# Two transformer blocks: the normed inputs move from VectorE to ScalarE, under a new work order

## The chip, the cores and the metric

The kernel runs on one core of a Trainium2 chip. A core has five engines with a queue of instructions each: TensorE (PE in the profile; PEld is its loading of weights), VectorE (DVE), ScalarE (ACT), GpSimd (POOL) and SyncE (SP), which here issues all DMAs. Each queue runs in order, and an instruction that waits for another engine holds up everything behind it. The metric is the device time in microseconds, as the median of several runs. Three runs of the kernel before gave 1454.73, 1455.28 and 1455.34 us.

## The reference, cut to what matters

A batch of 32 sequences of 128 tokens with 256 features goes through two blocks, all in fp32. Each block is self attention, cross attention to a context, and a feed-forward part of width 1024, with 16 heads of 16 features. In front of each of the three parts the input is normed over its features:

```python
m = jnp.mean(x, axis=-1, keepdims=True)
v = jnp.mean((x - m) ** 2, axis=-1, keepdims=True)
return (x - m) / jnp.sqrt(v + EPS)
```

Most of these normed inputs are then scaled by a factor `1 + scale` and shifted, both taken from a condition vector. There are 6 norms for each sequence, three in each block.

## The kernel before

The 32 sequences are handled as 16 groups of two (`GB = 2`), so a tile of inputs `x` is 128 tokens by 2 x 256. Every group goes through both blocks. Eight streams (`NS`) are under way at once, each with one group, so that while one stream waits for a transfer or for a softmax the products of another run. Five sets of query, key and value tiles (`NA`), three tiles for normed inputs (`y`), four tiles of PSUM for products and a single one for scores are shared by all the streams.

The order of the work is not the order of the code. A planner in the kernel (`Clock` and `Tasks`) runs while the program is built. Every step of a stream is a Python generator that yields when it can start, on which engine and with which shared tiles. The planner keeps a time for each engine, picks the step to issue next, and adds the cost that the step states with `clock.use`. In each stretch of 40 us of planned time the number in `ORDER` decides how long it holds back for a step of better rank, and stirs the ranks. So the costs in `clock.use` and the numbers in `ORDER` decide the order in which the instructions of all streams stand in each engine's queue. On the chip these queues are fixed, and the engines wait for one another by semaphores. They do not keep the planned times.

The steps that the prediction speaks of are these:

- **The norm** (`normed_T`, L565 to L588). VectorE takes the mean and variance `mv` of each sequence with bn_stats and bn_aggr (L572, L573). GpSimd adds eps (L577) and raises to the power -0.5 (L579), which gives `rstd`. Two operations, one for each sequence, then write the normed tile `y` (L586). TensorE transposes it in four pieces (`transposed`, L598), and ScalarE or VectorE, whichever is planned to be free first, scales and shifts it out of PSUM into the stream's tile `xt` (L616 on ScalarE, L618 on VectorE).
- **Attention** (`attention`, from L751). For each sequence TensorE computes the scores (L761), VectorE takes the largest of each row (L773), TensorE transposes these (L786), VectorE subtracts them from the queries (L790, tile `qa`), TensorE computes the scores anew (L761), ScalarE takes the exponential (L799), and TensorE multiplies by the values (L807). ScalarE copies the result to a tile `ou` (L813), some of whose rows hold the sums of the exponentials.
- **The division by the sums** (`over_sums`, L818 to L842). The sums go by DMA to a tile `few` (L825), the other rows to `xt` (L827), VectorE inverts `few` (L830), the inverses go by DMA to DRAM (L833) and by two more DMAs back to where they are needed (L838), and VectorE multiplies (L841). After this come the output projection (`project`, with `w_sa_out_w` or `w_ca_out_w`) and the sum with `x` (L881, or L885 and L889 where there is a gate).
- **Setting up** (`set_up`, L391). ScalarE fills the five sets' query and key tiles, ten copies of 128 x 1024, once, at the start.
- **Products** (`multiply`, L273 and L275). A product with a weight is one matmul of 128 columns, or four of 32 columns, where the planner finds TensorE already working in parts.

Of the kernel before, what the change touches and what calls it, by code (L numbers as in the profile page):

```python
# [10 lines left out]
F32 = mybir.dt.float32  # L11
U8 = mybir.dt.uint8
AF = mybir.ActivationFunctionType
ALU = mybir.AluOpType
# [3 lines left out]
P = 128  # L18
B, S, D, H, HD, DF = 32, 128, 256, 16, 16, 1024
KC = D // P  # L20
FC = DF // P
GB = 2
# [10 lines left out]

EVERY = 40.0
ORDER = (
    38718, 32014, 0, 87893, 99950, 56838, 0, 53341, 21925, 7768, 6954, 0, 63578, 91846, 41557, 5424, 0, 45477, 0,
    75801, 0, 86349, 57432, 99928, 14485, 81598, 5044, 38730, 0, 40902, 37263, 32089, 83999, 84738, 0, 0, 0
)


# [201 lines left out]
def two_blocks(ctx: ExitStack, tc: tile.TileContext, a: dict, out: bass.AP):  # L242
    nc = tc.nc

    def pool(name, bufs, **kw):
        return ctx.enter_context(tc.tile_pool(name=name, bufs=bufs, **kw))
# [5 lines left out]
    clock = Clock()  # L252
# [14 lines left out]
    p_s = pool("p_s", NS + 2)  # L267
# [297 lines left out]
    def normed_T(wm, x, ready, eps, mod, g, name):  # L565


        mv = p_s.tile([P, GB, 2], F32, tag="mv", name=f"mv_{name}")
        yield ready, "dve", "", 1
        for b in range(GB):  # L570
            st = p_s.tile([P, 6], F32, tag="st", name=f"st_{name}_{b}")
            nc.vector.bn_stats(st, x[:, b, :])  # L572
            nc.vector.bn_aggr(mv[:, b, :], st)  # L573
        t = clock.use("dve", 1.17)
        yield t, "pool", "", 1
        ve = p_s.tile([P, GB], F32, tag="ve", name=f"ve_{name}")
        nc.gpsimd.tensor_scalar(ve, mv[:, :, 1], eps, None, ALU.add)  # L577
        rstd = p_s.tile([P, GB], F32, tag="rstd", name=f"rstd_{name}")
        nc.gpsimd.tensor_tensor(rstd, ve, neg_half, ALU.pow)  # L579
        t = clock.use("pool", 1.0)  # L580
        yield t, "dve", "y", 0
        y = clock.take("y")
        xn = ys[y]
        for b in range(GB):

            nc.vector.scalar_tensor_tensor(xn[:, b, :], x[:, b, :], mv[:, b, 0:1],  # L586
                                           rstd[:, b:b + 1].to_broadcast([P, D]), ALU.subtract, ALU.mult)
        t = clock.use("dve", 0.75)  # L588
        return (yield from transposed(wm, y, t, mod, g))

    def transposed(wm, y, t, mod, g):
        to, xn = wm.xt, ys[y]
        yield (lambda: when(t) if mod is None or mod in mods else NEVER), "pe", "mm", 1
        slot = clock.take("mm")
        ps = mms[slot].rearrange("p (c b s) -> p c b s", c=KC, s=S)
        for c in range(KC):
            for b in range(GB):
                nc.tensor.transpose(ps[:, c, b, :], xn[:, b, c * P:(c + 1) * P], ident)  # L598
        t = clock.use("pe", 0.45, "turned")
        clock.give("y", y, t)  # L600
        there = Event()

        def evict():

            engine = "act" if mod is None else clock.freer("act", "dve")
            yield t, engine, "", 1
            if mod is None:
                nc.scalar.copy(to.rearrange("p c (b s) -> p c b s", s=S), ps)
            else:
                scale, shift = mods[mod]  # L610
                for c in range(KC):
                    for b in range(GB):
                        at = g * GB + b
                        one, by, to_add = to[:, c, b * S:(b + 1) * S], scale[:, c, at:at + 1], shift[:, c, at:at + 1]
                        if engine == "act":
                            nc.scalar.activation(one, ps[:, c, b, :], AF.Identity, bias=to_add, scale=by)  # L616
                        else:
                            nc.vector.tensor_scalar(one, ps[:, c, b, :], by, to_add, ALU.mult, ALU.add)  # L618
            clock.give("mm", slot, there.add(clock.use(engine, 0.6 if mod is None else 1.45)))

        tasks.spawn(evict(), wm)
        return there
# [128 lines left out]
    def attention(wm, hd, masked, t, t_v, name, done):  # L751
# [66 lines left out]
        def over_sums():  # L818


            n, w = 4 * R, 4 * H * GT // P
            yield copied, "sp", "", 1
            o = ous[ou[0]]
            few = p_s.tile([P, w], F32, tag="few", name=f"few_{name}", bufs=3)
            nc.sync.dma_start(out=few, in_=o[1:P:8, :, :])  # L825
            at = clock.dma(2.0)
            nc.sync.dma_start(out=wm.xt, in_=o[0:P:2, :, :])  # L827
            clock.dma(2.4)
            yield at, "dve", "", 1
            nc.vector.reciprocal(few, few)  # L830
            yield clock.use("dve", 1.15), "sp", "", 1
            inv = dram2.tile([n, C * GT], F32, tag="inv", name=f"inv_{name}")
            nc.sync.dma_start(out=inv.rearrange("r (t w) -> (r t) w", w=w), in_=few)  # L833
            yield clock.dma(1.5), "sp", "", 1
            by = o[:, 0:KC, :]
            for c in range(2):
                half = inv[:, c * KC * GT:(c + 1) * KC * GT]
                nc.sync.dma_start(out=by[c:P:2, :, :], in_=half.unsqueeze(1).to_broadcast([n, 4, KC * GT]))  # L838
                at = clock.dma(2.3)
            yield at, "dve", "", 1.5  # L840
            nc.vector.tensor_tensor(wm.xt, wm.xt, by, ALU.mult)  # L841
            clock.give("ou", ou[0], done.add(clock.use("dve", 0.7)))  # L842

        copied = Event(GB)
        for b in range(GB):
            tasks.spawn(batch(b), wm)
        tasks.spawn(over_sums(), wm)
        yield last, "none", "", 0
        return last
# [97 lines left out]
    def attended(wm, at, x, masked, t, t_v, w, bias, gate, eps, mod, g, name, then, cx=None):  # L947

        done = Event()
        end = yield from attention(wm, heads[at], masked, t, t_v, name, done)  # L950
        if cx is not None:
            tasks.spawn(cx.fetch(wm), wm)
        if masked:
            end = yield from mask_row(heads[at], zeros, 0)
        clock.give("set", at, when(end))
        if gate is not None:
            gate = yield from load_gate(wm, gate, g)
        t = yield from project(wm, x, lambda k, b: wm.xt[:, k, b * S:(b + 1) * S], KC, w, done, bias, gate, name)
        return (yield from normed_T(wm, x, t, eps, mod, g, then))
# [55 lines left out]
    def stream(wm, mine, loaded):  # L1015

        while loaded:
            first, g = wm.group < NG, wm.group % NG
            x, tx = loaded
            t = yield from normed_T(wm, x, tx, 1e-6 if first else 1e-5, ("L0", "sa") if first else ("L1", 1), g,  # L1020
                                    f"{'a' if first else 'd'}{g}")
            t = yield from (first_block if first else second_block)(wm, x, t, g)
# [125 lines left out]
```

## Time and profile before

| | |
|---|---|
| Median of three runs | 1455.28 us |
| Profiled execution, whole time | 1451.29 us |
| Its span, first to last instruction | 1449.5 us |
| Granted TensorE clock, mean | 0.995 |
| TensorE busy | 98% of the span |
| VectorE busy | 62% |
| ScalarE busy | 48% |
| GpSimd busy | 25% |
| Norm, write of `y` on VectorE (L586) | 192 operations, 128 x 256 each, median 480 ns |
| Inverse deviation on GpSimd (L577, L579) | 96 of 217 ns and 96 of about 705 ns, medians |

The profile is of one execution. The durations of single instructions and the waits are read from it, and they add up to its span. A busy TensorE is not a TensorE at its peak, since matmuls are pipelined and their ends are modelled. The chain of work that ended last runs 82% of the span over TensorE:

```profile
PE 82%; DVE 6%; DMA 5%; issue 2%; POOL 2%; ACT 1%; SPq 1%; DVEq 0%; ACTq 0%; POOLq 0%
```

The idle time of an engine other than TensorE costs nothing by itself. It matters where TensorE waits for that engine.

### The profile page before, as it was taken

The page shows a single profiled execution, that of the slowest core. Times are in us where ns is not written, and L with a number is a line of the kernel's source. Part 1 is how long each engine was busy: PE and PEld are TensorE (multiplying, and loading weights), DVE is VectorE, ACT ScalarE, POOL GpSimd, SP SyncE. Part 2 cuts the span into 40 slices and gives each one's busy share as a digit, 9 for nine tenths or more (in the row PEclk, how much of TensorE's full clock was granted, in tenths as well). Part 3 has the DMA queues.
Part 4 walks back from the last instruction along what each step waited for, and adds up shares of the span by engine and source line. Part 5 has one row for each costly group of instructions (what it writes and reads, how often), then busy time and mean ns, then how long its engine had stood idle before and what let it go on. Part 6 is the DMA issues. An engine that isn't in the chain of part 4 may idle for free.

```text
span 1449.5 us, 45874 instructions
## 1 busy us (share of the span) xinstructions
PE 1422.2 (98%) x20160; PEld 1124.9 (78%) x20160; DVE 900.0 (62%) x1546; ACT 701.1 (48%) x1120; POOL 363.6 (25%) x498
## 2 busy tenths in 40 slices
PE   8999999999999999999999999999999999999998
PEld 7777788777878787787877877778778777768777
DVE  6766656755665565647456665886486567684541
ACT  6554545555446444554455354444444444445542
POOL 3222223213314232424223221222221112210111
PEclk9999999999999999999999999999999999999999
DMA  7432213313132313223322422231121121321110
GB/s 224 155 93 88 72 57 103 100 50 105 46 90 75 108 59 104 89 60 111 99 71 75 151 75 82 85 103 61 60 81 64 56 89 53 96 83 45 42 53 22
DMA packets 107384, 120.91 MB, mean 83 GB/s; under 512 B 11632, under 2 KB 82992, under 8 KB 107184
## 3 DMA queue, kind: packets, MB, share of 16 engines
q1 hardware_dynamic: 107184, 117.98, 25.8%
q8 instruction: 158, 2.59, 0.7%
q14 instruction: 42, 0.34, 0.1%
HBM read 54.92 MB, written 12.68 MB: 47 GB/s over the span
## 4 chain that ended last, share of the span: by engine, by line
PE 82%; DVE 6%; DMA 5%; issue 2%; POOL 2%; ACT 1%; SPq 1%; DVEq 0%; ACTq 0%; POOLq 0%
PE products L275 42%; PE scores L761 16%; PE products L273 13%; PE products L807 7%; PE products L598 3%; DVE top L773 2%; PE products L786 1%; DVE y L586 1%; ACT exp L799 1%; DMA few_b<-ou 1%; DVE qa L790 1%; DMA ou<-inv_b 1%; POOL x L867 1%; POOL gb_a L866 1%; DVE st L736 0%
## 5 line engine op out<-in xcount | busy, mean ns | idle before, releaser
L773 DVE TENSOR_REDUCE top<-scores 128x8 f32<-128x1024 f32 x256 | 300.4, 1215 | 66.8 <-PE scores L761 58.9
L799 ACT ACTIVATE exp<-scores 128x1024 f32<-128x1024 f32 x256 | 248.4, 1023 | 150.5 <-PE scores L761 144.2
L275 PE MATMUL products<-w_ffn_w,ht 128*128 128x256 f32 x896 | 202.4, 381 | 0.0
L275 PEld LDWEIGHTS products<-w_ffn_w,ht 128*128 128x128 f32 x896 | 167.6, 190 | 23.6
L905 ACT ACTIVATE ht<-products,cols 128x256 f32<-128x256 f32 x256 | 115.7, 474 | 115.8 <-PE products L275 84.0
L275 PE MATMUL products<-xt,w_ffn_w 128*128 128x256 f32 x720 | 165.2, 382 | 0.5 <-ACT xt L616 0.5
L761 PEld LDWEIGHTS scores<-qa,keys 32*128 32x128 f32 x4096 | 125.9, 186 | 46.0 <-issue 19.8
L813 ACT COPY ou<-products 128x512 f32<-128x512 f32 x128 | 75.4, 589 | 178.0 <-PE products L807 177.7
L761 PEld LDWEIGHTS scores<-keys,queries 32*128 32x128 f32 x4096 | 126.6, 187 | 37.8 <-issue 21.9
L761 PE MATMUL scores<-qa,keys 32*128 32x128 f32 x4096 | 150.2, 283 | 4.4 <-ACT exp L799 1.6
L761 PE MATMUL scores<-keys,queries 32*128 32x128 f32 x4096 | 151.1, 284 | 2.6 <-ACT exp L799 1.3
L275 PEld LDWEIGHTS products<-xt,w_ffn_w 128*128 128x128 f32 x720 | 134.2, 191 | 20.9 <-ACT xt L616 1.3
L807 PE MATMUL products<-exp,values 128*32 128x128 f32 x4096 | 136.5, 275 | 0.2 <-ACT exp L799 0.2
L741 POOL TENSOR_TENSOR st<-st 128x512 f32<-128x512 f32 x64 | 83.6, 1309 | 204.8 <-DVE st L736 204.8
L790 DVE TENSOR_TENSOR qa<-queries,products 128x512 f32<-128x512 f32 x128 | 86.4, 677 | 72.7 <-PE products L786 55.5
L807 PEld LDWEIGHTS products<-exp,values 128*32 128x32 f32 x4096 | 105.7, 109 | 18.9 <-issue 6.0
L881 DVE TENSOR_TENSOR x<-products,x 128x512 f32<-128x512 f32 x64 | 43.9, 686 | 120.1 <-PE products L275 97.8
L275 PE MATMUL products<-xt,w_qkv_w 128*128 128x256 f32 x408 | 99.4, 389 | 0.8 <-DVE xt L618 0.8
L889 POOL TENSOR_TENSOR x<-y,x 128x512 f32<-128x512 f32 x32 | 41.1, 1285 | 216.2 <-DVE y L885 216.2
L656 ACT COPY values<-products 128x512 f32<-128x512 f32 x64 | 40.4, 632 | 111.8 <-PE products L275 62.8
L841 DVE TENSOR_TENSOR xt<-xt,ou 128x512 f32<-128x512 f32 x64 | 46.2, 723 | 74.5 <-DMA ou<-inv_e 20.6
L736 DVE TENSOR_TENSOR st<-products,rope 128x512 f32<-128x512 f32 x128 | 81.3, 679 | 7.8 <-ACT ou L813 3.3
(129 smaller groups left out, 1958.0 us busy)
## 6 DMA issues: line engine op xcount, KB each, us to landing
xt<-ou SPq DMA_DIRECT2D x64, 256.0 KB
keys<-st SPq DMA_DIRECT2D x96, 128.0 KB
queries<-st SPq DMA_DIRECT2D x96, 128.0 KB
cxt<-in_ctx SPq DMA_DIRECT2D x32, 256.0 KB
x<-in_x SPq DMA_DIRECT2D x16, 256.0 KB
keys<-st SPq DMA_DIRECT2D x16, 256.0 KB
y<-gate_dram_sa SPq DMA_DIRECT2D x16, 256.0 KB
ou<-inv_a SPq DMA_DIRECT2D x32, 128.0 KB
```

The lines of the kernel that those rows point to most:

```text
L273: nc.tensor.matmul(to[j:j + 32], lhsT=lhs[:, j:j + 32], rhs=rhs, start=start, stop=stop)
L275: nc.tensor.matmul(to, lhsT=lhs, rhs=rhs, start=start, stop=stop)
L736: nc.vector.tensor_tensor(st[:, :, :, one], ps[:, :, one].unsqueeze(2).to_broadcast([P, 2, 2, S]), rope, ALU.mult)
L741: nc.gpsimd.tensor_tensor(st[:, 0], st[:, 0], st[:, 1], ALU.add)
L761: nc.tensor.matmul(sc[:, r, c * S:(c + 1) * S], lhsT=lhs(slice(32 * r, 32 * r + 32), c), rhs=rhs(slice(32 * r, 32 * r + 32), c), start=Tru ...
L773: nc.vector.tensor_reduce(top[:, r:r + 2, TOP:TOP + 2 * C:2], scs[slot][:, r:r + 2, :].rearrange("p r (c s) -> p r c s", s=S), AX.X, ALU.max)
L790: nc.vector.tensor_tensor(qa, q[:, :, cut], ps.unsqueeze(1).to_broadcast([P, C, S]), ALU.subtract)
L799: nc.scalar.activation(exps[pt][r // 2], scs[slot][:, r:r + 2, :], AF.Exp, scale=SCALE)
L807: nc.tensor.matmul(mms[at][32 * r:32 * r + 32, c * S:(c + 1) * S], lhsT=v[:, b, i:i + HD, :].rearrange("p d t -> p (d t)"), rhs=exps[pt][r ...
L813: nc.scalar.copy(ous[ou[0]][:, :, cut], mms[at].rearrange("p (c s) -> p c s", s=S))
L841: nc.vector.tensor_tensor(wm.xt, wm.xt, by, ALU.mult)
L905: nc.scalar.activation(ht[f // (FC // 2)][:, f % (FC // 2), :], ps[:, 0, :], AF.Gelu, bias=b1[:, f:f + 1])
```

## The change

There are three edits. First, the normed tile is written by ScalarE in place of VectorE. ScalarE's activation computes `func(scale * x + bias)` with one scale and one bias for each row, so `(x - mean) * rstd` is written as `rstd * x + (-mean * rstd)`. GpSimd works out the bias `nmr`, with two more small operations, and the step's stated costs follow (1.45 for GpSimd, 0.9 for ScalarE). Second, the stated cost of the reciprocal in `over_sums` goes from 1.15 to 1.0; no instruction changes there. Third, the numbers in `ORDER` are others. Through the planner the second and third edits, and the costs of the first, change the order of the instructions in all queues.

```diff
 ORDER = (
-    38718, 32014, 0, 87893, 99950, 56838, 0, 53341, 21925, 7768, 6954, 0, 63578, 91846, 41557, 5424, 0, 45477, 0,
-    75801, 0, 86349, 57432, 99928, 14485, 81598, 5044, 38730, 0, 40902, 37263, 32089, 83999, 84738, 0, 0, 0
+    66186, 45635, 0, 5614, 0, 97056, 0, 0, 45817, 0, 76306, 2557, 0, 5440, 68618, 56612, 0, 0, 5688, 98877, 44020,
+    42862, 35677, 88006, 530, 79523, 1240, 10900, 26993, 41257, 0, 57405, 7496, 0, 55418, 19974, 0
 )
...
         rstd = p_s.tile([P, GB], F32, tag="rstd", name=f"rstd_{name}")
         nc.gpsimd.tensor_tensor(rstd, ve, neg_half, ALU.pow)
-        t = clock.use("pool", 1.0)
-        yield t, "dve", "y", 0
+        nmr = p_s.tile([P, GB], F32, tag="nmr", name=f"nmr_{name}")
+        nc.gpsimd.tensor_scalar(nmr, mv[:, :, 0], -1.0, None, ALU.mult)
+        nc.gpsimd.tensor_tensor(nmr, nmr, rstd, ALU.mult)
+        t = clock.use("pool", 1.45)
+        yield t, "act", "y", 0
         y = clock.take("y")
         xn = ys[y]
         for b in range(GB):
-
-            nc.vector.scalar_tensor_tensor(xn[:, b, :], x[:, b, :], mv[:, b, 0:1],
-                                           rstd[:, b:b + 1].to_broadcast([P, D]), ALU.subtract, ALU.mult)
-        t = clock.use("dve", 0.75)
+            nc.scalar.activation(xn[:, b, :], x[:, b, :], AF.Identity, bias=nmr[:, b:b + 1], scale=rstd[:, b:b + 1])
+        t = clock.use("act", 0.9)
         return (yield from transposed(wm, y, t, mod, g))
...
             nc.vector.reciprocal(few, few)
-            yield clock.use("dve", 1.15), "sp", "", 1
+            yield clock.use("dve", 1.0), "sp", "", 1
```

## The prediction

> **What bounds the kernel now.** I read the page's busy shares first, then TensorE's waits, then the timelines of the places that these point to.
>
> ```profile
> PE 1422.2 (98%) x20160; PEld 1124.9 (78%) x20160; DVE 900.0 (62%) x1546; ACT 701.1 (48%) x1120; POOL 363.6 (25%) x498
> ```
>
> TensorE is busy for 1422.2 of 1449.5 us, so only 27.3 us can be won or lost by anything that does not change TensorE's own stream. Of these, 3.6 us lie at the start (1.35 + 1.46 + 0.82 in the timeline of the first 12 us) and about 4 after the last product (it ends at 1445.5; an add and a store follow). Some 19.7 us in the middle remain, of which the waits by engine name 18.1. The largest are:
>
> ```profile
> PE products L598 <- DVE y L586: 5.4, 8, 1.5
> PE products L275 <- DVE xt L841: 4.9, 5, 1.9
> PE scores L761 <- ACT exp L799: 2.9, 4, 1.1
> PE products L786 <- DVE top L778: 1.7, 4, 0.6
> PE scores L761 <- DVE qa L790: 1.5, 1, 1.5
> PE scores L761 <- DVE top L773: 1.2, 3, 0.6
> ```
>
> (microseconds in total, times, longest.) The change moves exactly L586, so its first line is what it can remove: 5.4 us, of which 1.46 belong to the start. But the second half of the change, a new ORDER, replaces the order of every instruction, so all the other lines are dealt anew.
>
> **What the Trainium skill says.** (1) "ScalarE: Activation LUTs", section "What ACT_TABLE_LOAD costs": an ACTIVATE with a pointer bias takes about 280 ns + 0.833 ns per element, 93 more for a second pointer operand, and neighbours overlap by 93. For 256 columns with bias and scale pointers that is 586 ns alone and, as an estimate, 0.49 apiece in a row. The trace agrees: L682, the same form on 256 columns out of PSUM, has a mean of 566 ns. (2) The same page, "Table sets: the hidden batching unit", has identity in every set. In the trace 228 Identity evictions of L616 and L682 share ScalarE with 32 + 32 loads for exp and gelu alone, so the new ones bring no load. (3) "SBUF — State Buffer", "Who interferes with whom": a VectorE operation with two SBUF inputs contends with GpSimd reads, and ScalarE waits on no one. The trace agrees: L586 has a median of 480 ns but a mean of 509 to 656 by group, and this pair, beside a bias add of GpSimd, took 1.82 us in place of 0.88:
>
> ```profile
> 1403.37 1.82 DVE L586 SCALAR_TENSOR_TENSOR y<-x,mv_f,rstd_f 128x256 f32<-128x256 f32 x2 [1.13 <-POOL rstd_f L579]
> ```
>
> **The change, part by part.**
>
> *TensorE's stream.* The compiled instruction orders of the two kernels, set side by side, hold the same products. The new one issues about as many of them in four 32-column parts (2056 matmuls of that form against 2096), and that would cost nothing, since four parts take as long as one whole product (0.216 us a pass either way, start to start in the timeline). A turn between forms costs 0.1 us from whole products to scores, 0.1 back, 0.11 out of parts or exp products, 0 from exp products to parts; counted with these, the turns of the old order come to 50.1 us and of the new to 50.9. **+0.7.**
>
> *VectorE loses* 192 operations, 106.7 us (15.0+19.5+19.7+17.0+18.6+16.9 in the groups of L586), and takes 16 more evictions (140 for 124) of 0.34: 900 becomes about 799. *ScalarE gains* 192 x 0.49 = 94, and sheds 16 evictions (6 us) and 6 table loads of 1.283 (7.7; 29 + 29 in the new order): 701 becomes about 781. *GpSimd* gains 192 tiny operations. The multiply by -1 is of L577's kind (217 ns, next one 0.30 later); a 128x2 product is not in the trace: between 0.22 (L577) and 0.70 (the pow of L579), I take 0.25, that is 0.6 for the pair and 58 us in all on an engine that is 75% idle. SyncE issues the same 567 rows in another order.
>
> *The norm's chain* is thus 0.6 (GpSimd) + about 0.1 (a pair of 0.98 against 0.88 unhindered) longer, and shorter by up to 0.9 where GpSimd stood in the way. What counts is the queue ahead of y: reductions of 2.35 us before, exps of 1.94 now. I placed each kernel's TensorE order on a line with the pitches above, and asked for each y whether the last reduction (or exp) ahead of it, plus what lies between, ends in time for L598. Shortfalls add to 3.6 us before (3.9 measured after the start) and 0.6 now: **-3.0**. Behind a y that waits for its nmr stand exps, gelus and evictions on ScalarE, and TensorE's next scores or products behind them; 0.97 a time where nothing covers it. I take nothing for it, since reductions lose the same 0.98 behind y on VectorE today.
>
> *The start.* In the new ScalarE order six fills of queries and keys (L391) stand ahead of the first y. They run from 5.40, 0.945 apart:
>
> ```profile
> 5.40 1.04 ACT L391 COPY queries<-rows 128x1024 f32<-128x1024 f32 x1 [2.54 <-DMA rows<-in_rows]
> 6.35 1.04 ACT L391 COPY keys<-rows 128x1024 f32<-128x1024 f32 x1
> ```
>
> So y begins at 5.40 + 6 x 0.945 = 11.07, its first half is there at 11.65, and the first transposition, which came at 9.23 behind VectorE's y of 8.70, moves by **+2.45**. Nothing else is there for TensorE to do: the same 12 warm-up products and modulations stand ahead of it.
>
> *The round of scores.* The same question for reduction to transposition, to the next scores, to qa, and exp to its products: shortfalls sum to 13.9 before and 18.6 now, neighbours counted twice. Several lie between 36 and 70 us and at 766, 1004 and 1064; before they lay around 1250. I take under half of the difference: **+2**.
>
> *The sums' round trip* (L825 to L841) has no cover but other streams' products. Its latency, from the last exp product to the multiplied xt, I read from all 64 cases: the shortest are 9.2, 9.8 and five of 10.0 to 10.2, the lower quartile is 11.7. One that stalled:
>
> ```profile
> 1247.31 0.69 DVE L841 TENSOR_TENSOR xt<-xt,ou 128x512 f32<-128x512 f32 x1 [2.30 <-DMA ou<-inv_d]
> ```
>
> ```profile
> 1241.78 1.08 PE L807 MATMUL products<-exp,values 128*32 128x128 f32 x32
> ...
> 1248.14 1.19 PE L275 MATMUL products<-w_sa_out_w,xt 128*128 128x256 f32 x2 [1.91 <-DVE xt L841]
> ```
>
> (L841 waited 2.30 us for its DMA, and TensorE 1.91 for L841.) The other edit tells the planner that L830 takes 1.0 in place of 1.15 (0.94 measured). In the old order the least work between exp products and projection is 10.5, 10.7 and then 11.9 us; in the new 8.9, 9.0, 9.4, 9.7, 9.8, 10.3, 10.5, and eight more below 11.4. At a latency of 10.2 five of them fall short, by 1.3+1.2+0.8+0.5+0.4: **+4.2**. At 9.2 it would be 0.5, at 11.7 it would be 17 more than before. I take 10.2, about the mean of the seven shortest, since these were the ones with nothing in their way.
>
> *VectorE's relief elsewhere.* L841's 4.9 us of waits came at places with room for 10.5 or more, so from queues on VectorE, GpSimd or SyncE. With 11% less on VectorE I take **-1.5**; no row shows it, between 0 and -4.
>
> Sum: 0.7 - 3.0 + 2.45 + 2 + 4.2 - 1.5 = **+4.9**; 1449.5 becomes 1454.4. The profiled execution took 1451.3 in all, and the median of the runs is 1455.3, 5.8 above the span; so 1460.3, say **1460**.
>
> **The rivals.**
> *Faster.* VectorE's relief is the whole story: the norm's 3.9 us go, half of L841's 4.9, and the 3.4 lost to exp and top (L799, L773) from 1276 to 1309, where the new order has no such pile of scores; start and turns cost 3.15. That is -6.6, **1449**. It holds if the sums' trip stays at 9.2 to 9.4 where it is short of cover, and decides from there. For: VectorE is named for 13.2 of 18.1. Against: nearly all short covers got shorter.
> *No change.* Gaps move, their sum doesn't; what the norm gives back, start and turns take: 0.7+2.45-3.0 = 0, **1455.5**.
> *Slower by more.* The trip takes its quartile of 11.7 also where it is short: 17 us, of which a third is shared with other waits; with the rest of the sum, less its 4.2, that is about +12, **1467**. For: queues on SyncE (DMAs of other streams ahead of L833 and L838) are as before.
>
> **How the numbers follow.** Forecast (+2.9 to +9) 0.40, slower by more 0.14, no change 0.20, faster 0.26. A measurement here tells about 0.2% (2.9 us). Faster 0.26, same 0.20, slower 0.54. The forecast's own range is 1458 to 1465; to leave out no more than 2 in 10, 1449 to 1468.
>
> **What would show it.** In the profile after: L598's first start near 11.65; waits on y near 1 us after the start; no VectorE y at all; ScalarE near 781 busy, VectorE near 799, 58 table loads for exp and gelu; TensorE's busy time within 2 us of 1422; and "products L275 (or L273) <- DVE xt L841" as the largest wait, at 8 us or more. If that line stays below 5 us, the forecast is wrong and the faster rival right; if the start is not late, the six fills did not stand in y's way.

## The result, and the profile after

The kernel after the change takes 1464.77 us in the median of seven runs (1460.75 to 1469.46), beside 1455.93 (1454.73 to 1460.12) for seven runs of the kernel before on the same chip. The ratio is 1.0059, with a 95% interval of 1.0041 to 1.0077. It is slower by 0.6%, where the forecast was 0.3%.

The profiled execution took 1466.39 us with a span of 1464.3, so it lies 1.6 above the median, while the one of before lay below its own. The two spans differ by 14.8 us, the medians by 8.8. What follows accounts for the 14.8, so its parts hold for these two executions, and together they are 6 us more than the medians show. First the busy times, from the page of after:

```profile
PE 1423.7 (97%) x20100; PEld 1127.4 (77%) x20100; DVE 804.6 (55%) x1370; ACT 779.4 (53%) x1290; POOL 393.9 (27%) x690
```

TensorE's own work is nearly what it was (1422.2). VectorE lost 95 us and ScalarE gained 78, as reckoned. So the time went into waits of TensorE. This is the view of TensorE's waits after the change (total, times, longest):

```profile
PE products L275 <- DVE xt L842: 9.2, 8, 2.5
PE products L599 <- ACT y L588: 6.4, 5, 4.3
PE scores L762 <- DVE top L774: 3.6, 5, 1.9
PE products L273 <- DVE xt L842: 3.0, 3, 1.5
PE products L787 <- DVE top L774: 2.9, 4, 1.1
PE products L275 <- ACT ht L906: 2.2, 2, 1.4
PE scores L762 <- DMA queries<-st: 1.7, 1, 1.7
PE scores L762 <- DMA keys<-st: 1.5, 3, 0.8
PE products L273 <- ACT ht L906: 1.0, 1, 1.0
PE scores L762 <- ACT exp L800: 0.7, 2, 0.5
```

(The write of y is L588 now, in place of L586, and line numbers behind it are one higher than in the kernel before.) Set against the waits of before:

| What TensorE waits for | before, us | after, us |
|---|---|---|
| first y of the kernel | 1.5 | 4.3 |
| other y | 3.9 | 2.1 |
| xt, at the end of the sums' round trip | 4.9 | 12.2 |
| round of scores: top, qa, exp | 7.8 | 7.5 |
| gelu output or its release of a PSUM tile (ht) | 0.5 | 3.2 |
| queries and keys by DMA | 0.4 | 3.2 |
| TensorE busy | 1422.2 | 1423.7 |

The differences add to 15.0 us of the 14.8. Half of it is the round trip alone.

The timeline of the longest wait on the trip shows its legs:

```profile
1022.97 1.06 PE L808 MATMUL products<-exp,values 128*32 128x128 f32 x32
...
1024.09 0.58 ACT L814 COPY ou<-products 128x512 f32<-128x512 f32 x1 [2.92 <-PE products L808]
1024.70 0.58 SPq L826 DMA_DIRECT2D few_e<-ou  x1
...
1026.74 0.95 DVE L831 RECIPROCAL few_e<-few_e 128x128 f32<-128x128 f32 x1 [2.76 <-DMA few_e<-ou]
...
1027.72 0.34 SPq L834 DMA_DIRECT2D inv_e<-few_e  x1
...
1030.95 1.20 SPq L839 DMA_DIRECT2D ou<-inv_e  x2
...
1034.59 0.69 DVE L842 TENSOR_TENSOR xt<-xt,ou 128x512 f32<-128x512 f32 x1 [2.00 <-DMA ou<-inv_e]
...
1035.42 2.04 PE L275 MATMUL products<-w_ca_out_w,xt 128*128 128x256 f32 x4 [2.46 <-DVE xt L842]
```

The exp products end at 1024.03, and the multiplied xt is there at 1035.28, 11.25 us later. VectorE itself works for 0.95 + 0.69 of these, and ScalarE's copy for 0.58. The rest is transfers and their issue. The last line shows a further cost: its four matmuls took 2.04 us. Four of the same form elsewhere in this trace took half of that:

```profile
1170.48 1.03 PE L275 MATMUL products<-w_ca_out_w,xt 128*128 128x256 f32 x4
```

From 1035.03 to 1038.44 the granted clock of TensorE, the share of full speed that it was allowed, was 0.50 (1.00 in the microseconds before the wait). There are three such stretches of 3.41 us in this profile after the start, and two in that of before (a third lies behind its last product). The last section comes back to them.

L842 also held up VectorE for 2.00 us, with a reduction behind it. This cost has its own row in the groups of VectorE. The first line is from the page of before, the second from the groups of after; the number behind the mean is the idle time just before it:

```profile
L841 DVE TENSOR_TENSOR xt<-xt,ou 128x512 f32<-128x512 f32 x64 | 46.2, 723 | 74.5 <-DMA ou<-inv_e 20.6 <-DMA ou<-inv_a 19.4 <-DMA ou<-inv_b 17.8
```

```profile
L842 DVE TENSOR_TENSOR xt<-xt,ou 128x512 f32<-128x512 f32 x64 | 46.2, 721 | 110.5 <-DMA ou<-inv_a 30.1 <-DMA ou<-inv_b 25.2 <-DMA ou<-inv_d 21.2
```

VectorE stood 74.5 us in front of these 64 multiplications before and 110.5 after. It is idle for much of the span anyway, but whatever is queued behind the multiplication waits too.

### The profile page after: what moved, and what is told of

Its sections match the earlier page's. It is cut to its first block, busy times and chain, and to the rows that moved or that the text cites. A ratio compares the mean times of both kernels' runs of the same rounds, so it can differ in the third digit from the quotient of the medians.

```text
span 1464.3 us, 46030 instructions
## 1 busy us (share of the span) xinstructions
PE 1423.7 (97%) x20100; PEld 1127.4 (77%) x20100; DVE 804.6 (55%) x1370; ACT 779.4 (53%) x1290; POOL 393.9 (27%) x690
## 4 chain that ended last, share of the span: by engine, by line
PE 80%; DMA 8%; DVE 5%; ACT 3%; POOL 2%; issue 2%; SPq 1%; DVEq 0%; POOLq 0%; ACTq 0%
PE products L275 41%; PE scores L762 15%; PE products L273 12%; PE products L808 7%; PE products L599 3%; DVE top L774 1%; PE products L787 1%; DMA inv_e<-few_e 1%; DMA ou<-inv_e 1%; ACT exp L800 1%; DMA keys<-st 1%; DMA few_d<-ou 1%; SPq L839 1%; ACT y L588 1%; DMA inv_b<-few_b 1%
## 5 line engine op out<-in xcount | busy, mean ns | idle before, releaser
L275 PE MATMUL products<-xt,w_ffn_w 128*128 128x256 f32 x768 | 176.5, 383 | 2.3 <-ACT ht L906 2.2
L275 PE MATMUL products<-w_ffn_w,ht 128*128 128x256 f32 x784 | 177.8, 382 | 0.0
L275 PEld LDWEIGHTS products<-w_ffn_w,ht 128*128 128x128 f32 x784 | 146.6, 190 | 21.6
L275 PEld LDWEIGHTS products<-xt,w_ffn_w 128*128 128x128 f32 x768 | 142.8, 190 | 24.0 <-ACT ht L906 3.0
L842 DVE TENSOR_TENSOR xt<-xt,ou 128x512 f32<-128x512 f32 x64 | 46.2, 721 | 110.5 <-DMA ou<-inv_a 30.1
L275 PE MATMUL products<-xt,w_qkv_w 128*128 128x256 f32 x360 | 87.3, 389 | 0.8 <-DVE xt L619 0.8
L886 DVE TENSOR_TENSOR y<-products,y 128x512 f32<-128x512 f32 x32 | 22.0, 689 | 110.1 <-PE products L275 60.7
```

The source lines that it names most:

```text
L275: nc.tensor.matmul(to, lhsT=lhs, rhs=rhs, start=start, stop=stop)
```

## The experiments

Each ratio is to the kernel before, run on the same chip in the same session, with its 95% interval. The profiles are single executions.

| Kernel | ratio | interval |
|---|---|---|
| after the change | 1.0059 | 1.0041 to 1.0077 |
| old order, y on ScalarE | 1.0158 | 1.0144 to 1.0171 |
| new order, y on VectorE | 1.0236 | 1.0223 to 1.0249 |
| after, first y on VectorE | 1.0042 | 1.0028 to 1.0056 |
| after, no wait for the trip | 0.9919 | 0.9905 to 0.9933 |
| before, no wait for the trip | 0.9942 | 0.9925 to 0.9960 |
| y on ScalarE, trip +1.0, searched | 0.9984 | 0.9975 to 0.9992 |
| y on VectorE, trip +1.0, searched | 1.0032 | 1.0019 to 1.0044 |
| y on either, trip +1.0, searched | 0.9998 | 0.9984 to 1.0011 |
| y on ScalarE, trip +0, searched | 1.0167 | 1.0147 to 1.0188 |
| y on ScalarE, trip +1.0, wider search | 0.9949 | 0.9932 to 0.9966 |
| y on ScalarE, trip +1.8, wider search | 0.9861 | 0.9843 to 0.9879 |
| y on VectorE, trip +1.8, wider search | 0.9932 | 0.9913 to 0.9951 |

### Engine and order apart

The theory was that the new order lost the time and the engine did not. The rival was that ScalarE's fuller queue costs by itself. Since the planner reckons with stated costs only, the order of all steps can be kept while another engine is given the work. In the first kernel the planner of before is untouched:

```diff
         nc.gpsimd.tensor_tensor(rstd, ve, neg_half, ALU.pow)
+        nmr = p_s.tile([P, GB], F32, tag="nmr", name=f"nmr_{name}")
+        nc.gpsimd.tensor_scalar(nmr, mv[:, :, 0], -1.0, None, ALU.mult)
+        nc.gpsimd.tensor_tensor(nmr, nmr, rstd, ALU.mult)
         t = clock.use("pool", 1.0)
         yield t, "dve", "y", 0
...
-            nc.vector.scalar_tensor_tensor(xn[:, b, :], x[:, b, :], mv[:, b, 0:1],
-                                           rstd[:, b:b + 1].to_broadcast([P, D]), ALU.subtract, ALU.mult)
+            nc.scalar.activation(xn[:, b, :], x[:, b, :], AF.Identity, bias=nmr[:, b:b + 1], scale=rstd[:, b:b + 1])
         t = clock.use("dve", 0.75)
```

> The old order of all steps is kept (the planner reckons as before); only the engine that writes the normed tile changes, with the two operations for its bias on GpSimd. Theory (the loss is the new order's, not the engine's): the late start costs 2.8 us here too, since six fills stand ahead of the first y, the waits on y after the start fall from 3.9 to about 1, and VectorE's relief gives 1 to 2; so 1453 to 1457, not told from before. Rival (ScalarE's fuller queue is what costs): waits on ScalarE (exp, ht) grow by 5 us or more, 1461 or more.

In the second kernel the planner of after is untouched, the two nmr operations are gone, and VectorE's operation is back.

> The new order of all steps is kept (the planner reckons as after the change); the normed tile is written by VectorE as before, without the bias. Theory: the start is early again (-2.8), but the waits on the sums' trip (xt from L842) stay at 10 to 14 us and waits on y come back (about 3); 1462 to 1467, as slow as after the change. Rival (the engine is what costs): back to 1455 to 1458.

Both expectations fell. With the old order and y on ScalarE the kernel is 1.6% slower than before, with the new order and y on VectorE 2.4% slower. TensorE's waits in the first of them, and then in the second:

```profile
PE products L600 <- ACT y L589: 16.9, 32, 3.3
PE products L275 <- DVE xt L843: 5.1, 4, 2.5
```

```profile
PE products L597 <- DVE y L585: 14.6, 16, 1.7
PE products L275 <- DVE xt L840: 13.4, 14, 2.5
PE products L273 <- DVE xt L840: 4.2, 5, 1.0
```

The waits on y grow to about 15 us in both, which fits two orders that were each made for one engine. The waits on xt go with the order, though: 5.4 with the old one (0.3 of it at L273) in place of 4.9, though the engine of y has changed, and 12.2 or 17.6 with the new one. So neither theory holds whole. An order is worth what it is only for the placement that it was made for. But the trip's short cover belongs to the new order. ("New order" here means all of the change but the engine: the numbers in `ORDER`, the stated costs and the shorter stated reciprocal. These were not taken apart.) Whether the engine is good or bad can't be seen from these two. It needs two kernels searched alike, which come below.

### The start

```diff
         for b in range(GB):
+            if name == "a0":
+                nc.vector.scalar_tensor_tensor(xn[:, b, :], x[:, b, :], mv[:, b, 0:1],
+                                               rstd[:, b:b + 1].to_broadcast([P, D]), ALU.subtract, ALU.mult)
+                continue
             nc.scalar.activation(xn[:, b, :], x[:, b, :], AF.Identity, bias=nmr[:, b:b + 1], scale=rstd[:, b:b + 1])
```

> After the change, but the very first normed tile (group 0, first block) is written by VectorE, so that it doesn't stand behind six fills. Theory: TensorE's first transposition is at 9.2 in place of 11.6 us and the whole kernel 2.4 to 2.8 us shorter, about 1462. Rival (the delay is taken up by later waits, such as those of the loads): no more than 1 us shorter.

The delay itself is plain in the timelines. After the change ScalarE and TensorE start so:

```profile
10.01 1.04 ACT L391 COPY keys<-rows 128x1024 f32<-128x1024 f32 x1
10.96 1.09 ACT L588 ACTIVATE y<-x,nmr_a,rstd_a 128x256 f32<-128x256 f32 x2
```

```profile
11.61 1.39 PE L599 MATMUL products<-ident,y 128*128 128x128 f32 x4 [4.26 <-ACT y L588]
```

and with only the first y moved back, TensorE starts so:

```profile
9.77 0.94 PE L603 MATMUL products<-ident,y 128*128 128x128 f32 x4 [0.90 <-DVE y L589]
```

That is 1.84 us earlier, though not at the 9.2 that was expected. The ratio went from 1.0059 to 1.0042, or 2.5 us, but the intervals overlap, so the effect on the whole is likely and not shown.

### The trip's wait alone

In both kernels the division by the sums is left out. The inverses are fetched to a tile of their own, and the multiplication stays:

```diff
-            by = o[:, 0:KC, :]
+            by = p_b.tile([P, KC, GT], F32, tag="by", name=f"by_{name}")
...
-            nc.vector.tensor_tensor(wm.xt, wm.xt, by, ALU.mult)
+            nc.vector.tensor_tensor(wm.xt, wm.xt, rope.rearrange("p a b s -> p a (b s)"), ALU.mult)
```

> After the change, with the division by the sums left out: the inverses are fetched all the same, to a tile that nobody reads, and xt is multiplied by the rope table, so that all instructions and transfers stay and only the wait for the inverses goes. Theory: the 12.2 us that TensorE waits for xt from L842 go, and with L842 no longer holding up VectorE some of the waits on top go too: 12 to 16 us shorter, 1449 to 1453. Rival (waits only move on to the next release, the score rounds): 6 us or less.

> Before the change, with the division by the sums left out in the same way: the inverses go to a tile that nobody reads and xt is multiplied by the rope table. Theory (the old order covers the sums' trip better): 4.9 us of waits on xt go, and a few on top behind them, 5 to 9 us shorter than before, so much less than the 20 us that the same edit gave in the new order. Rival (the trip costs both orders alike, and the new order loses elsewhere): 15 us or more.

From the new order this took 1.40% (1.0059 to 0.9919), some 20 us. From the old order it took 0.58%, some 8. The difference, 0.82%, is more than the 0.59% that the change cost. Without this one wait the new order is no slower than the old. Both gains exceed TensorE's listed waits on xt (12.2 and 4.9, of which 0.4 is left in each). In the new order other waits fell too, those on top, as the theory had it, and those on the queries' and keys' DMAs (3.2 to 1.1). In the old order no other wait fell by more than 0.5; there TensorE's busy time fell, from 1422.2 to 1419.8, and its clock stood at half for 6.8 us in place of 13.7. TensorE's waits and VectorE's group in the new order without the trip's wait:

```profile
PE products L600 <- ACT y L589: 5.1, 5, 3.3
PE scores L763 <- DVE top L775: 2.5, 4, 1.0
```

```profile
L843 DVE TENSOR_TENSOR xt<-xt,rope 128x512 f32<-128x512 f32 x64 | 51.5, 806 | 0.0
```

The idle time in front of the multiplication is gone (110.5 to 0.0), and the waits on top fell from 6.5 to 4.1 in this profile (2.5 here, 1.6 at the transposition). The theory holds. Its size was above what was expected in the new order (20 us for 12 to 16) and within it in the old (8 for 5 to 9). This profile is of the slowest of the kernel's six runs, 1450.59 us beside a median of 1442.85: the clock stood at half for 17.1 us from 50.7 on.

### Orders searched anew, with a longer trip stated

If the stated costs make the trip too short, the planner should do better when told the truth. Three kernels state 1.0 us more for the trip, and what the profile shows for y and its bias. Their ORDER was searched with the planner itself, stretch by stretch of 40 us, keeping the 5 beginnings that get most of TensorE's work done and trying 30 numbers on each. Of each setting one order was run, the best by plan of a few searches. One has y on ScalarE (but the first), one on VectorE, one on the engine that is planned free first. The core of the first:

```diff
+        engine = "dve" if name == "a0" else "act"
-        yield t, "act", "y", 0
+        yield t, engine, "y", 0
...
-        t = clock.use("act", 0.9)
+        t = clock.use(engine, 0.98)
...
-            yield clock.dma(1.5), "sp", "", 1
+            yield clock.dma(1.5) + 0.50, "sp", "", 1
...
-            yield at, "dve", "", 1.5
+            yield at + 0.50, "dve", "", 1.5
```

> Normed tiles on ScalarE, except the very first; the planner is told that the sums' trip takes 1.0 us longer, 0.98 for a pair of y and 1.6 for GpSimd's part, and ORDER is searched for these costs. The shortest covers of the trip are 10.3, 10.7, 10.8 and 11.3 us in place of 8.9, 9.0, 9.4 and 9.7. Theory (short cover and the late start are what lost): waits on xt fall to 5 us or less, start at 9.2, so 1447 to 1453, as fast as before or faster. Rival (y on ScalarE costs by itself): 1458 or more, whatever the order.

> Normed tiles on VectorE as before; the same longer trip, 0.98 for a pair of y and 1.0 for the reciprocal told to the planner, and ORDER searched in the same way and for as long. It is the fair partner of the kernel with y on ScalarE. Theory (VectorE's relief is worth 1 to 4 us at equal search): 2 to 5 us slower than that one, 1450 to 1456. Rival (the engine makes no difference): within 2 us of it.

> As the one with y on ScalarE, but each y goes to whichever of VectorE and ScalarE the planner has free first. The shortest covers of the trip are 11.4, 11.6, 11.7 and 11.8 us. Theory: waits on xt at 4 us or less, 1447 to 1453. Rival (VectorE's y meets GpSimd's reads again, and the plan is missed there): slower than the kernel with all y on ScalarE by 3 us or more.

With y on ScalarE the kernel is a little faster than before (0.9984), and TensorE's waits on xt are 5.5 us in place of 12.2, just above the 5 expected. So the rival that y on ScalarE costs by itself, whatever the order, falls. Its partner with y on VectorE is slower (1.0032, a median of 1459.56 us, above the 1450 to 1456 expected). ScalarE is ahead by 0.48%, about 7 us. But TensorE's waits on xt in the partner are only 0.7 us, less than the 5.5 of the faster kernel. It lost the time elsewhere: 6.0 us on y, 8.1 on top, and 4.7 in one wait on qa. So a covered trip isn't enough, and what the search gives up in its place differs from one order to the next. The mixed kernel is at 0.9998, 2 us behind the one on ScalarE. Its waits on xt were 5.3 us, above the 4 expected, and its time is within what was expected.

The next three tell apart the trip's stated length and the width of the search: the same kernel with the trip as the change had it (width as above), with 1.0 us and a wider search (8 beginnings, 40 numbers), and with 1.8 us and the wider search (`+ 0.90` in both places).

> The same kernel with the trip's stated length left as in the change under study, y's costs as in the other two, and ORDER searched with the first search's width and seed. The shortest covers are 9.9, 10.5, 10.8, 11.0 and 11.1 us, between those of the change (8.9, 9.0, 9.4) and those at 1.0 longer (10.3, 10.7, 10.8). Theory: 2 to 5 us of waits on xt more than at 1.0 longer, 1452 to 1458. Rival (the search's luck decides and the stated length does not): within 1 us of the one at 1.0 longer, or faster.

> As the kernel with y on ScalarE and the trip 1.0 longer, with the wider search of the one at 1.8. The shortest covers are 9.9, 10.4, 10.9 and 11.0 us. It tells apart what the wider search gives and what the longer stated trip gives. Theory: 3 us or more slower than at 1.8 longer. Rival (it is the width): within 2 us of it.

> As the kernel with y on ScalarE (the first on VectorE) and ORDER searched, but the planner is told that the sums' trip takes 1.8 us longer in place of 1.0, and the search was about twice as wide. The shortest covers of the trip are 12.7, 12.9, 12.9 and 12.9 us. Theory (the trip's cover decides): no wait on xt beyond 2 us in all, 1443 to 1450, faster than before by 0.3% or more. Rival (longer cover for the trip takes it from other steps): waits on y, top and exp grow by as much, 1451 or more.

The ratios are 1.0167, 0.9949 and 0.9861. At the first width the kernel with 1.0 us more stated is ahead of the one with none by 1.8%; at the second width the one with 1.8 is ahead of the one with 1.0 by 0.9%, as the theory had it; at the same trip the wider search is ahead by 0.35%. Each is a difference between two single orders. Waits on xt don't explain the first: they differ by 1.1 us. And the shortest covers of the wider search at 1.0 (9.9 and 10.4 us) are shorter than those of the narrower one (10.3 and 10.7), while its waits on xt are fewer, 2.2 us for 5.5. At 1.8 the kernel is faster than before by 1.4%, more than was expected. TensorE's largest waits in it, and the group of the multiplication:

```profile
PE products L605 <- ACT y L591: 3.8, 5, 2.1
PE scores L768 <- ACT exp L806: 2.3, 2, 2.1
PE products L276 <- ACT ht L912: 1.7, 3, 0.9
```

```profile
L848 DVE TENSOR_TENSOR xt<-xt,ou 128x512 f32<-128x512 f32 x64 | 47.1, 738 | 44.1 <-DMA ou<-inv_e 11.9 <-DMA ou<-inv_a 11.3 <-DMA ou<-inv_d 7.4
```

No wait of TensorE on the multiplied xt is left at all, and VectorE's idle time in front of it is 44.1 us. In the kernels with y on ScalarE and an order made for it, this idle time goes roughly with the span: 44.1 (span 1436.3), 60.3 (1449.5, wider search at 1.0), 72.4 (1450.0), 102.4 (1475.9, trip not lengthened), 110.5 (1464.3, the change). With y on VectorE it does not: 74.5 (1449.5, before), 49.2 (1459.4, trip at 1.0), 25.9 (1446.7, the last kernel below).

The kernel with the trip not lengthened did not fail in the way that was expected. Its waits:

```profile
PE products L605 <- ACT y L591: 13.9, 14, 3.9
PE scores L768 <- DVE top L780: 5.0, 4, 2.4
PE products L276 <- DVE xt L848: 4.2, 5, 1.5
...
PE products L274 <- DVE xt L848: 2.4, 3, 1.7
```

Only 6.6 us are on xt, 1 more than at 1.0, and 13.9 are on y. Around 637 us the timeline of this kernel shows how one of these y came to be late:

```profile
631.60 0.73 POOL L873 TENSOR_TENSOR gb_a<-y,r_sa 128x256 f32<-128x256 f32 x1 [12.80 <-DMA y<-gate_dram_sa]
...
634.69 0.22 POOL L578 TENSOR_SCALAR ve_d<-mv_d 128x2 f32<-128x2 f32 x1
...
636.31 1.09 ACT L591 ACTIVATE y<-x,nmr_d,rstd_d 128x256 f32<-128x256 f32 x2 [9.87 <-POOL nmr_d L583]
...
636.96 0.33 PE L605 MATMUL products<-ident,y 128*128 128x128 f32 x1 [3.90 <-ACT y L591]
```

The mean and variance of this norm were there at 628.86 (the end of its second bn_aggr), but GpSimd stood until 631.60 for a gate's rows, and four operations on gates went ahead of the norm's. So here a transfer for the gates held up another queue. That the trip's stated length brings this about, and not the draw of this search, is not shown.

Last, the partner of the best kernel, with y on VectorE, the trip at 1.8 and the same wider search:

> The partner of the kernel with y on ScalarE and the trip stated 1.8 us longer: normed tiles on VectorE, the same stated trip, the same width and seed of the search. The shortest covers of the trip are 11.7, 12.6, 12.8 and 13.8 us. Theory (most of the gain is the trip's cover, but VectorE's relief is worth a few us at equal search): faster than before by 0.3 to 1%, 1443 to 1453, and 5 to 12 us slower than with y on ScalarE. Rival (the engine doesn't matter once the trip is covered): within 3 us of 1437.

It is faster than before too, at 0.9932, and 0.71% behind the one on ScalarE, within what the theory had. Its largest wait is

```profile
PE products L599 <- DVE y L587: 10.3, 7, 3.5
```

the wait on y (3.0 of it at the start), which stands at 3.8 (and 0.9 for the first) with ScalarE. In both pairs that were searched alike the kernel with y on ScalarE is ahead, by 0.5 and 0.7%. That the engine gives this is likely and not shown, since two orders for one engine, at one stated trip, differ by 0.35% themselves. What is shown is that the loss of the change is its order's: under other orders the kernel with y on ScalarE, all but the first, is faster than before.

The version to keep is the one with y on ScalarE and the trip at 1.8, at 0.9861. Its numbers:

```python
ORDER = (
    65504, 68093, 18002, 59037, 0, 17956, 0, 0, 0, 12934, 33012, 77522, 0, 89913, 96438, 68805,
    99944, 95884, 84340, 0, 0, 78190, 57512, 26145, 62220, 59842, 11261, 17096, 2932, 53778, 9450, 44717,
    0, 55416, 0, 0, 0
)
```

## Why the prediction was right

The sign was right, and so was the term that was to be the largest. The size, +0.33% forecast and +0.59% measured, is within the range, though only just: 1464.77 us, with the range's end at 1465. In part that is luck. The terms gave +4.9 for the span, where the two profiles differ by 14.8 and the medians by 8.8, and the errors below do not all go one way. By its own steps:

- *TensorE's stream*, +0.7: TensorE is busy for 1.5 us more. This doesn't show that the turns did it: its clock stood at half for 17.1 us in place of 13.7, which by itself comes to about 1.7 us (an estimate, half of the 3.4 us more).
- *Engine loads*: VectorE at 799 reckoned and 804.6 measured, ScalarE 781 and 779.4, 58 table loads for exp and gelu. The price of a pair of y on ScalarE, 0.98, was low by a tenth: each takes 583 to 629 ns and a pair 1.09 in the timelines. The unknown product on GpSimd was taken as 0.25 and is 0.194, and GpSimd is busy for 30 us more, not 58.
- *The norm's chain*, -3.0: the waits on y after the start fell from 3.9 to 2.1, -1.8; near 1 was expected.
- *The start*: the first transposition was forecast at 11.65 and came at 11.61.
- *The round of scores*, +2: it came to -0.3. Waits on top grew by 3.6 and those on exp and qa fell by 3.9. My count of shortfalls took the first and gave too little for the second.
- *The sums' round trip* is the term that was mis-sized. The sum had +4.2 for it, less part of the 1.5 for VectorE's relief, so 8 us or so in all; it was 12.2. In the trace of after, with each multiplication paired to its own trip by the order of the issues, five of the eleven waits, 7.1 us in total, stand behind trips of 10.4 to 11.3. These are the short covers, priced at 4.2. The other six, 5.2 us, stand behind longer trips of 11.9 to 16.3, as all five of before did (13.8 to 17.9, 4.9 us). In these six 2.9 to 4.8 us went by from the issue of the first transfer to the reciprocal; in the one shown it was 2.0. So the latency of 10.2 was too short. It isn't the mean of the seven shortest either, which is 9.9 (at that the same sum gives 2.7); it is the longest of them. The lower quartile of 11.7, the price of the rival "slower by more", would have been too long (17 us more than before).
- *VectorE's relief elsewhere*, -1.5: not seen; the waits behind the longer trips stayed (4.9 before, 5.2 after). The waits on ht and on the queries' and keys' DMAs, which no step of the prediction named, grew by 5.5 us in its place.

The rival "faster" was decided where the prediction put it: the trip did not stay at 9.2 to 9.4 where it was short of cover. But it fell for this order, and not for y on ScalarE as such, since other orders with it are faster than before. What the prediction did not see is that a transfer that comes late costs more than TensorE's wait for the multiplication: what VectorE has queued behind it waits too, and TensorE's clock can stand at half behind a long wait.

## What to carry to other kernels

Judge a move of work between engines only with an order made for it on both sides: with its order kept, the same move cost 1.6% here, and in two pairs searched alike it was ahead by 0.5 and 0.7%. Run more than one order of each setting, since two orders for one engine at one stated trip differed by 0.35%. Where a planner fixes in-order queues ahead of time, state the round trips over DMA as long as they are under load and not as short as they can be; the best kernel here, 1.4% faster than before in place of 0.6% slower, has 1.8 us more on one stated latency, beside a wider search, new costs for y and the first y on VectorE. And look at what an engine's queue holds behind an instruction that waits for a transfer: with the trip's wait gone, the time fell by more than TensorE had been seen to wait for it.

## What the runs showed of the hardware

Long waits of TensorE go with a lower clock behind them. In the fourteen profiles, past the first 20 us, TensorE waited for 2.46 us or longer twelve times. At each of the twelve its granted clock was 0.50 for a stretch of 3.41 or 6.83 us, which began during the wait or within 2 us of its end. Of the forty waits between 1.0 and 1.4 us two had one, and of those in between some. The longest stretch, 17.1 us, had only a wait of 0.6 us ahead of it, so these waits are not the only way to it. In it the 32 matmuls of a round of scores took 1.97 us, where they take 1.17 at full clock.

With one and the same order of TensorE's instructions, its busy time was not constant: 1422.2 us before, 1429.8 with y moved to ScalarE under the old order. Of the 7.6 us between them, 1.7 can be the clock (an estimate: 17.1 us at half in place of 13.7). The rest was not traced. A comparison by idle time alone misses all of it. The write of y on ScalarE took 583 to 629 ns in all six norms of the profile after, beside whatever GpSimd did, where VectorE's took 405 to 1498 before.
